# Seven block products for layer 0's values, their sums on GpSimd, and a later load of x

## The chip, the cores and the metric

The kernel runs on one core of a Trainium2 chip. A core has a matrix engine (TensorE, PE in the profile; PEld are its weight loads), a vector engine (VectorE, DVE), an engine for pointwise functions (ScalarE, ACT), a general one (GpSimd, POOL) and one that here only issues transfers (SyncE, SP). Each works through its own instructions in order and waits on semaphores for the others. Matrix products land in PSUM, everything else lies in SBUF. The metric is the device time of one execution in microseconds, as the median over several runs.

## What is computed

Two attention blocks on x of shape (8, 512, 32, 32): eight elements, 512 channels, 1024 tokens. Everything is fp32. Cut to what matters:

```python
# layer 0, heads of 64 channels
hn = group_norm(x, gn1_scale, gn1_bias)
qkv = einsum('bchw,oc->bohw', hn, w_qkv) + b_qkv      # q, k, v
wgt = softmax(einsum('bct,bcs->bts', q * scale, k * scale))
a = einsum('bts,bcs->bct', wgt, v)
x = x + group_norm(einsum('bchw,oc->bohw', a, w_proj) + b_proj, gn2_scale, gn2_bias)
# layer 1, one head of 512 channels
qkv = einsum('oc,bcn->bon', w_qkv1, x);  qkv = qkv / rms(qkv)
h = softmax(q^T k / sqrt(512)) applied to v
x = (x + einsum('oc,bcn->bon', w_out, h)) / sqrt(2)
```

The change concerns v of layer 0, the product of the normalized input hn (512 channels by 1024 tokens) with 512 x 512 weights.

## The kernel before

The elements go one after the other, and of two neighbours the stages overlap. For one element b there are these stages.

**Steps.** A loop of 32 steps (lines 1151 to 1215; STEPS = 32, NB = 8 steps for each of four pairs of heads). A step takes 128 tokens of one pair of heads. Heads.step (line 595) writes out the order: the softmax of step i (a maximum on VectorE, the exponential on ScalarE), every second step values() (TensorE: probabilities times v for an earlier group of two steps), the fills (mostly a projection for the next pair of heads), the scores of step i + 1 on TensorE, turn() (VectorE transposes the probabilities of step i − 1 in blocks of 32, SP sends them on in four transfers into the buffer pT), scale() (GpSimd multiplies the probabilities of step i by their reciprocal sums), and last the list `later`. The probabilities' transposed tiles pb have two buffers, so a transposition waits until the transfers of two steps before have landed.

**Drain.** Lines 1217 to 1241 and finish_layer0 (line 781): the last two values(), the last turn(), then the output projection with its group norm and the residual. Into it the values of the next element are laid as fills for TensorE: project_v0 (line 505) yields eight pieces, each the four 128x512 matmuls of 128 tokens against the weights near["v"], with one copy by ScalarE for two pieces. One piece stands ahead of values(14), three ahead of values(15), the other four in finish_layer0 around the norm's small matmuls. The output projection's weights proj7 are fetched behind the last turn(); x's four loads are issued in steps 28 and 30 and two ahead of values(15).

**Layer 1.** Layer1.project (line 840) starts with the products py of x and the matrix gram, goes on with the score units, the value units and the weight units; then come the products with e and the output.

Several matrix products are made from seven block products instead of eight (class Seven, line 697; in the manner of Strassen and Winograd): an operand is cut into 2 x 2 blocks; the left sums S1 to S4 of the weights are prepared once in the prologue (operands, line 1043), the right sums T1 to T4 of the data are made by RightSide.sums (line 674), eight VectorE subtractions of 128x512. A unit is seven products of two matmuls each. Two products share one PSUM tile of two banks, and when both are issued, their drains follow: for the first product a copy by ScalarE, for the others adds on VectorE, two for the fifth. In the order of the products the fourth is A22 times T4. Before, layer 0's output projection, layer 1's scores, values and weights are made so; layer 0's values are not. Layer 0's projections for queries and keys have a form of their own (Sums and project_seven).

**What sets the order.** InOrder (line 26) pins every instruction in program order on its engine, and so SP's transfers too: what is written later waits behind what is written earlier. Big SBUF tiles come from seven slots (Slots, line 37): a slot given back goes to the end of the list, and the next taker waits for its last reader. Weights live in four named places of one buffer each (places, line 213): "qk", "v", "p" and parts of them; a fetch into a place waits for the last reader of what stood there. The PSUM pool ps_s has three tiles of two banks, tag "sc", which the scores, the seven-product pairs and py share in turn. In the place "v", 3,584 columns wide, near["v_"] is the part that holds v's weights and, at another time, sums of hn (t3); near["v#"] is the rest and serves as scratch space for project_rows and project_seven.

Of the kernel before, what the change touches and what calls it, by code (L numbers as in the profile page):

```python
# [13 lines left out]
P = 128  # L14
# [38 lines left out]
def attention_blocks_kernel(  # L53
# [153 lines left out]
    def rsqrt(r, v, n, name):  # L207
# [4 lines left out]
    CH = C // 2  # L212
    places = {
        "qk": ("qk", [P, 2, CI, C]), "score": ("qk", [P, 7, 2, CH]), "qk7": ("qk", [P, 2, 14, P]),
        "v": ("v", [P, 7, 2, CH]), "value": ("v", [P, 7, 2, CH]),
        "proj": ("p", [P, CI, C]), "gram": ("p", [P, CI, C]), "t24": ("p", [P, CI, HN]), "proj7": ("qk", [P, 7, 2, CH]),
    }
    far = {
        name: dram.tile([P, CI, C] if name == "v" else shape, F32, tag=f"far_{name}", name=f"far_{name}")
        for name, (_, shape) in places.items()  # L220
        if name not in ("qk", "t24", "qk7")
    }

    far["qk0"] = dram.tile([P, 2, CI, P], F32, tag="far_qk0", name="far_qk0")
# [4 lines left out]
    def place(name, b):  # L229
        tag, shape = places[name]  # L230
        near[name] = weights.tile(shape, F32, tag=f"w_{tag}", name=f"{name}_{b}")
        if name == "v":

            flat = near[name].rearrange("p k h c -> p (k h c)")
            near["v#"], near["v_"] = flat[:, CI * C :], flat[:, : CI * C]
            near[name] = flat[:, : CI * C].rearrange("p (ci c) -> p ci c", ci=CI)
        return near[name]
# [139 lines left out]

        return qk, pieces()

    def project_rows(b, j, hn):  # L380

        qk = pair.tile([P, 2, N], F32, tag="qk", name=f"qk_{b}_{j}")
        kp = qk[:, 1, :].rearrange("p (be m) -> p be m", be=4)
        spare = near["v#"]

        def pieces():
            for t in (1, 0):

                w = near["qk"][:, t, :, j * P : (j + 1) * P] if b < 2 else near["qk0"][:, t]
                bias = col(BK, j) if t else bqs[:, j : j + 1]
                for th in range(2):
                    hs = slice(th * HN, (th + 1) * HN)
                    pms = [bank(f"pqk_{b}_{j}_{t}_{th}_{r}") for r in range(2)]
                    for ci in range(CI):
                        for r in range(2):
                            PE.matmul(
                                pms[r],
                                w[halves[r], ci, :],  # L400
                                hn[halves[r], ci, hs],
                                start=(ci == 0),
                                stop=(ci == CI - 1),
                            )
                    to, rest = qk[:, 0, hs], spare[:, hs]
                    if t:

                        to = kp[:, :, th * P : (th + 1) * P]
                        rest = rest.rearrange("p (be m) -> p be m", be=4)
                        pms = [pm.rearrange("p (m be) -> p be m", be=4) for pm in pms]  # L410
                    AC.activation(to, pms[0], AF.Identity, bias=bias)
                    AC.copy(rest, pms[1])
                    yield [lambda to=to, rest=rest: PO.tensor_add(to, to, rest)], []

        return qk, pieces()
# [89 lines left out]
    def project_v0(b, hn, v):  # L505

        for t2 in range(NT // 2):
            pm = wide(f"pv0_{b}_{t2}")
            for k in range(2):
                t = 2 * t2 + k  # L510
                run(matmuls(pm[:, k, :], [(hn[:, ci, t * P : (t + 1) * P], near["v"][:, ci, :]) for ci in range(CI)]))
                if k:
                    AC.copy(v[:, 2 * t2 : 2 * t2 + 2, :], pm)
                yield

    class Heads:
        def __init__(self, b, hn, v, qk):
# [149 lines left out]
    class RightSide:  # L667
# [3 lines left out]
        def __init__(self, xt, t12, t34):  # L671
            self.xt, self.t12, self.t34 = xt, t12, t34

        def sums(self, j):

            xt, t12, t34 = self.xt, self.t12, self.t34
            m, (t1, t2) = j % 2, (slice(0, HN), slice(HN, N))
            if j < 2:
                VE.tensor_sub(t12[:, 0, m], xt[:, m, t2], xt[:, m, t1])
            else:  # L680
                VE.tensor_sub(t12[:, 1, m], xt[:, j, t2], t12[:, 0, m])
                VE.tensor_sub(t34[:, 0, m], xt[:, j, t2], xt[:, m, t2])
                VE.tensor_sub(t34[:, 1, m], xt[:, j, t1], t12[:, 1, m])

        def columns(self, cols):

# [94 lines left out]
    def finish_layer0(b, h, rhs, xt, v0):  # L781

        o, w = big(f"o_{b}"), near["proj7"]
        st = small.tile([P, CI, 2, 6], F32, tag="gn_st2", name=f"st2_{b}")
        mv = small.tile([P, CI, 2], F32, tag="gn_mv2", name=f"mv2_{b}")
        norm = GroupNorm(mv, CI, G2S, G2B, f"2_{b}")

        def unit(m):
            c = {
                f"{i + 1}{th + 1}": o[:, m + 2 * i, th * HN : (th + 1) * HN] for i in range(2) for th in range(2)  # L790
            }
            return Seven(
                f"o_{b}_{m}", HN,
                lambda k, hh: w[:, k, hh, m * P : (m + 1) * P], rhs.columns(slice(0, HN)), c, lambda which: None,
                bias=(col(BP, m), bpd[:, m : m + 1]),
            ).steps()

        def stats(j):
            for k in range(2):
                gn_stats(st[:, j], o[:, j, :], k)  # L800

        units = [unit(m) for m in range(2)]
        for u in units:
            next(u)

        for j in range(CI // 2 + 1, CI):
            rhs.sums(j)
        for m, u in enumerate(units):
            for k in range(6):
                next(u)  # L810
                if k == 3:
                    stats(m + 2)
            stats(m)
        slots.give(f"a_{b}")
        slots.give(f"ta_{b}")
        fetch("score", b)
        next(v0)
        for j in range(CI):
            VE.bn_aggr(mv[:, j, :], st[:, j])
        norm.means()  # L820
        next(v0)
        a, c = norm.coeffs()
        for j in range(CI):
            AC.activation(o[:, j, :], o[:, j, :], AF.Identity, bias=c[:, j : j + 1], scale=a[:, j : j + 1])
            VE.tensor_add(xt[:, j, :], xt[:, j, :], o[:, j, :])
        run(v0)
        slots.give(f"o_{b}")

    class Layer1:
# [188 lines left out]

    def turn_w0(t, name):
        turn(w0rows[t], near["v"] if t == 2 else near["qk"][:, t], name, QSCALE0 if t == 0 else 1.0)  # L1020
        if t == 2:
            SY.dma_start(out=far["v"], in_=near["v"])

    def operands_qk():

# [90 lines left out]
    turn_w0(2, "v")  # L1116
    for ci in range(CI):
        norm1.apply(ci, PO if ci % 2 else VE)
    operands("score", score, [block.tile([P, 4, 2, CH], F32, tag="pb", name=f"score7_{i}") for i in range(2)])
    for ci in range(CI):  # L1120
        AC.copy(value[:, ci, :], product(wv, [woT[:, o, :] for o in range(CI)], ci, "pB"))
# [26 lines left out]
    for b in range(B):  # L1148
        hn, more = heads.hn, b + 1 < B
        todo, due, rest = iter(()), [], []  # L1150
        for i in range(STEPS):
# [13 lines left out]
                fill, later = fills[i] + fill, laters[i]  # L1165
            if r == 0:
                if j + 1 < CI:
                    heads.qk[j + 1], todo = project_seven(b, j + 1, one.next.right) if b else project_rows(b, j + 1, hn)
                elif more:
                    qk_next, todo = project_rows(b + 1, 0, hn_next)  # L1170
                if j + 1 == CI:
                    slots.give(f"hn_{b}")
                    if not more:
                        o_last = big(f"o_{b}")
                        todo = project_out_half(b, heads, o_last)
# [28 lines left out]
            if b and i == STEPS - NB - 3 and not more:  # L1204
                fetch("proj", b)
            m, odd = divmod(i - STEPS + NB, 2)
            if b and more and m in (0, 1) and not odd:
                near["v"] = near["v_"].rearrange("p (ci c) -> p ci c", ci=CI)
                SY.dma_start(out=near["v"][:, 2 * m : 2 * m + 2], in_=far["v"][:, 2 * m : 2 * m + 2])

            if i == STEPS - 4:
                xt = big(f"x_{b}")
            if m in (2, 3) and not odd:
                load_x(b, xt, m - 2)
            heads.step(i, fill, early, later)

        if more:
            v0_next = big(f"v0_{b + 1}", NT)
            v0 = project_v0(b + 1, hn_next, v0_next)
            next(v0)  # L1220
        heads.values(STEPS // RG - 2)
        heads.turn()
        if more:
            fetch("proj7", b)
            if b:
                fetch("gram", b)
            ta = big(f"ta_{b}").rearrange("p (k i) (h n) -> p k i h n", k=2, h=2)
            rhs = RightSide(heads.a, ta[:, 0], ta[:, 1])
            for j in range(CI // 2 + 1):
                rhs.sums(j)  # L1230
            for _ in range(3):
                next(v0)
        else:
            fetch("score", b)
            begun = OutBegun(b, heads)
        for ci in (2, 3):
            load_x(b, xt, ci)
        heads.values(STEPS // RG - 1)
        slots.give(f"v0_{b}")
        if more:  # L1240
            finish_layer0(b, heads, rhs, xt, v0)
        else:
            finish_last(b, heads, xt, o_last, begun)
# [81 lines left out]
```

## Time and profile before

| | us |
|---|---|
| median of 3 runs | 3268.25 |
| lowest, highest | 3268.03, 3272.53 |
| profiled execution | 3268.6 |
| its span, first to last instruction | 3266.5 |
| mean granted TensorE clock | 0.998 |

The page gives for every engine the time in which it had work, then groups of like instructions: source line (all go through one helper, so all have line 34), engine, operation, output <- inputs, partitions x elements, count; behind the first bar the busy time in us and the mean length in ns; behind the second the idle time before them and what ended it. Tile names are short: pv is the PSUM tile of layer 0's values (and of the norm's second small matmul), po that of values(), p_o, p_u, p_v and p_e are the seven-product pairs of the output projection, the scores, the values and the weights, with _B for a product with a plain block and _T for one with a sum. A timeline line has the start in us, the length, the engine, the operation and the count of merged instructions. A line of a windows table has a stretch, its length, the busy time (and count) of PE, PEld, DVE, ACT and POOL, the granted clock, the busy share of the DMA engines and GB/s. The prologue ends at about 102 us; an element takes about 395 us.

Waits in total that touch the drain, from the table of waits: TensorE on pT's transfers 4.9 us in 5 places, VectorE's transposition on pT's transfers 24.6 us in 17.

### The profile page before, as it was taken

What the parts mean: (1) busy time and instruction counts of PE and PEld (TensorE: products, weight loads), DVE (VectorE), ACT (ScalarE), POOL (GpSimd) and SP (SyncE); (2) the same over time, 40 slices, a digit from 0 to 9 for tenths busy, and PEclk for the clock granted to TensorE, in tenths of its full rate; (3) what the DMA queues carried; (4) which work ended last, traced back from release to release, by engine and by line L of the source; (5) the groups of instructions that cost most, each with busy time, mean ns of one, the idle gap of its engine ahead of it and who ended that gap; (6) DMA issues with size and microseconds to landing.
All of it is one profiled execution on the core that took longest, in us unless ns stands there. A gap on an engine that the chain in (4) does not pass through costs nothing.

```text
span 3266.5 us, 35730 instructions
## 1 busy us (share of the span) xinstructions
PE 3235.1 (99%) x13010; PEld 1597.2 (49%) x13010; DVE 2229.7 (68%) x2982; ACT 1064.6 (33%) x1813; POOL 1127.6 (35%) x945
## 2 busy tenths in 40 slices
PE   8999999999999999999999999999999999999899
PEld 5444544445444454544544445444454545444354
DVE  5696667855678556885668756686667866568643
ACT  2453114521145211551215412254123531145210
POOL 0552124611256112660227503264123721246121
PEclk9999999999999999999999999999999999999999
DMA  6776215852168511783228822388214862157500
GB/s 190 212 202 171 74 48 155 220 179 58 49 181 224 164 42 55 205 230 121 52 77 213 228 84 58 98 217 235 73 50 113 216 201 74 23 155 211 180 7 26
DMA packets 228981, 438.88 MB, mean 134 GB/s; under 512 B 28708, under 2 KB 69192, under 8 KB 223048
## 3 DMA queue, kind: packets, MB, share of 16 engines
q1 hardware_dynamic: 228688, 436.58, 47.9%
q8 instruction: 104, 1.70, 0.2%
q14 instruction: 69, 0.57, 0.0%
q10 hardware_dynamic: 120, 0.02, 0.0%
HBM read 125.46 MB, written 28.74 MB: 47 GB/s over the span
## 4 chain that ended last, share of the span: by engine, by line
PE 90%; DMA 4%; DVE 3%; SPq 2%; issue 1%; POOL 0%; DVEq 0%; ACT 0%; ACTq 0%; POOLq 0%
PE po L34 25%; PE s L34 12%; PE pv L34 7%; PE p_e_T L34 7%; PE pq L34 6%; PE p_e_B L34 5%; PE py L34 4%; PE pqk L34 4%; DMA pT<-pb 4%; PE p_u_T L34 3%; PE p_v_T L34 3%; PE p_o_T L34 3%; PE p_v_B L34 3%; PE p_u_B L34 3%; PE p_o_B L34 2%; DVE pb L34 2%
## 5 line engine op out<-in xcount | busy, mean ns | idle before, releaser
L34 ACT ACTIVATE p<-s,nm 128x1024 f32<-128x1024 f32 x512 | 565.5, 1109 | 886.3 <-DVE nm L34 803.2
L34 POOL TENSOR_SCALAR p<-p,tt 128x1024 f32<-128x1024 f32 x512 | 565.9, 1118 | 812.7 <-DVE tt L34 798.4
L34 DVE TENSOR_REDUCE nm<-s 128x1 f32<-128x1024 f32 x512 | 602.3, 1218 | 160.2 <-PE s L34 160.0
L34 DVE STREAM_TRANSPOSE pb<-p 128x2048 f32<-128x2048 f32 x256 | 589.8, 2304 | 42.6 <-DMA pT<-pb 24.6
L34 PE MATMUL s<-qk 64*128 64x512 f32 x2048 | 523.6, 604 | 0.8 <-ACT p L34 0.2
L34 PE MATMUL po<-pT,v 128*64 128x256 f32 x4096 | 470.3, 382 | 4.9 <-DMA pT<-pb 4.9
L34 PE MATMUL po<-e,v 128*128 128x512 f32 x1024 | 451.7, 595 | 0.0
L34 PEld LDWEIGHTS po<-pT,v 128*64 128x64 f32 x4096 | 285.4, 137 | 227.2 <-ACT v L34 53.8
L34 POOL TENSOR_TENSOR u<-u,xy 128x512 f32<-128x512 f32 x64 | 78.9, 1269 | 764.5 <-DVE u L34 470.9
L34 PEld LDWEIGHTS s<-qk 64*128 64x128 f32 x2048 | 198.8, 186 | 252.0 <-issue 229.4
L34 PEld LDWEIGHTS po<-e,v 128*128 128x128 f32 x1024 | 191.9, 190 | 245.0 <-issue 236.4
L34 PE MATMUL pv<-v,hn 128*128 128x512 f32 x512 | 229.0, 598 | 0.0
L34 PE MATMUL pq<-hn,qk 64*128 64x512 f32 x504 | 197.1, 592 | 0.0
L34 ACT ACTIVATE e<-e,shift,rinv 128x512 f32<-128x512 f32 x128 | 100.9, 812 | 257.0 <-DVE e L34 257.0
L34 POOL TENSOR_TENSOR esum<-esum,e 128x512 f32<-128x512 f32 x96 | 130.4, 1360 | 154.2 <-ACT e L34 151.7
L34 DVE TENSOR_TENSOR e<-e,p_e_T 128x512 f32<-128x512 f32 x160 | 107.0, 685 | 86.9 <-PE p_e_T L34 84.7
L34 POOL TENSOR_TENSOR qk<-qk,v 128x512 f32<-128x512 f32 x124 | 162.8, 1320 | 3.2 <-ACT v L34 1.6
L34 PE MATMUL pqk<-hn,qk 64*128 64x512 f32 (+1 forms) x672 | 158.2, 590 | 0.0
L34 PEld LDWEIGHTS pv<-v,hn 128*128 128x128 f32 x512 | 94.6, 190 | 115.1 <-issue 114.3
L34 PE MATMUL pq<-t,qk 64*128 64x512 f32 x336 | 150.9, 589 | 0.0
L34 PE MATMUL pq<-v,qk 64*128 64x512 f32 x336 | 150.9, 589 | 0.0
L34 PE MATMUL p_e_T<-s,t 128*128 128x512 f32 x320 | 147.8, 592 | 0.0
(206 smaller groups left out, 3748.4 us busy)
## 6 DMA issues: line engine op xcount, KB each, us to landing
pT<-pb SPq DMA_DIRECT2D x1024, 256.0 KB, 4.6
qk<-far_qk SPq DMA_DIRECT2D x21, 896.0 KB, 8.2
hn<-in_x_dram SPq DMA_DIRECT2D x32, 512.0 KB, 6.1
x<-in_x_dram SPq DMA_DIRECT2D x32, 512.0 KB
out_dram<-x SPq DMA_DIRECT2D x32, 512.0 KB, 4.8
score<-far_score SPq DMA_DIRECT2D x8, 1792.0 KB
value<-far_value SPq DMA_DIRECT2D x8, 1792.0 KB, 7.5
proj<-far_proj SPq DMA_DIRECT2D x7, 1792.0 KB
```

The source lines that it names most:

```text
L34: return lambda *args, **kw: self._pin(call(*args, **kw))
```

## The change

Layer 0's values of the next element (elements 1 to 7) come from four units of seven products (project_v7), each product two matmuls of 128x256. v's weights are no longer stored as they are; operands() makes the seven left blocks "v7" in the prologue and stores them, and they are fetched whole, in four parts, in steps 24 to 27, also in element 0. The right sums of hn (tv, a slot taken at step 24) are made by GpSimd, one a step in the last eight steps, at the end of `later`. Of the 28 products, four stand ahead of values(14), ten ahead of values(15), four and two around the norm's means and two ahead of each of the four residual adds. Since v7 fills near["v#"] too, the scratch space of project_rows for the next element moves to a tile "spare" in place "p", and gram is fetched anew in element 0 as well. x's slot is taken, and its four loads issued, behind values(15); in the last element x stays as it was.

```diff
+        "spare": ("p", [P, N]),
...
+    def project_v7(b, right, v):
+
+        w = near["v7"]
+        for m in range(CI):
+            c = {f"{i + 1}{th + 1}": v[:, m + 4 * th, i * CH : (i + 1) * CH] for i in range(2) for th in range(2)}
+            yield from Seven(
+                f"v0_{b}_{m}", CH,
+                lambda k, h: w[:, k, h, :], right(slice(m * P, (m + 1) * P)), c, lambda which: None, swap=True,
+            ).steps()
...
-        def sums(self, j):
+        def sum_steps(self, j, engine=VE):
...
-                VE.tensor_sub(t12[:, 1, m], xt[:, j, t2], t12[:, 0, m])
-                VE.tensor_sub(t34[:, 0, m], xt[:, j, t2], xt[:, m, t2])
-                VE.tensor_sub(t34[:, 1, m], xt[:, j, t1], t12[:, 1, m])
+                engine.tensor_sub(t12[:, 1, m], xt[:, j, t2], t12[:, 0, m])
+                yield
+                engine.tensor_sub(t34[:, 0, m], xt[:, j, t2], xt[:, m, t2])
+                yield
+                engine.tensor_sub(t34[:, 1, m], xt[:, j, t1], t12[:, 1, m])
+                yield
...
         for j in range(CI):
             VE.bn_aggr(mv[:, j, :], st[:, j])
+        products(4)
         norm.means()
-        next(v0)
+        products(2)
         a, c = norm.coeffs()
         for j in range(CI):
+            products(2)
             AC.activation(o[:, j, :], o[:, j, :], AF.Identity, bias=c[:, j : j + 1], scale=a[:, j : j + 1])
             VE.tensor_add(xt[:, j, :], xt[:, j, :], o[:, j, :])
...
-            SY.dma_start(out=far["v"], in_=near["v"])
+    operands("v7", near["v"], [prob.tile([P, 4, 2, CH], F32, tag="p", name=f"v7_{i}") for i in range(2)])
...
-                    qk_next, todo = project_rows(b + 1, 0, hn_next)
+                    qk_next, todo = project_rows(b + 1, 0, hn_next, place("spare", b))
...
-            if b and more and m in (0, 1) and not odd:
-                near["v"] = near["v_"].rearrange("p (ci c) -> p ci c", ci=CI)
-                SY.dma_start(out=near["v"][:, 2 * m : 2 * m + 2], in_=far["v"][:, 2 * m : 2 * m + 2])
-
-            if i == STEPS - 4:
+            if more and m >= 0:
+                if m < 2:
+                    k = slice(2 * (i - STEPS + NB), min(2 * (i - STEPS + NB) + 2, 7))
+                    SY.dma_start(out=near["v7"][:, k], in_=far["v7"][:, k])
+                if i == STEPS - NB:
+                    tv = big(f"tv_{b + 1}").rearrange("p (k i) (h n) -> p k i h n", k=2, h=2)
+                    right_v = RightSide(hn_next, tv[:, 0], tv[:, 1])
+                    sums_v = (None for ci in range(CI) for _ in right_v.sum_steps(ci, PO))
+                later.append(lambda: next(sums_v, None))
...
+            v0 = project_v7(b + 1, right_v.columns, v0_next)
+            for _ in range(4):
+                next(v0)
         heads.values(STEPS // RG - 2)
         heads.turn()
         if more:
             fetch("proj7", b)
-            if b:
-                fetch("gram", b)
+            fetch("gram", b)
...
-            for _ in range(3):
+            for _ in range(10):
                 next(v0)
...
         heads.values(STEPS // RG - 1)
         slots.give(f"v0_{b}")
         if more:
+            xt = big(f"x_{b}")
+            for ci in range(CI):
+                load_x(b, xt, ci)
             finish_layer0(b, heads, rhs, xt, v0)
```

More of the change, by code (lines that the diff above doesn't have):

```diff
@@ L214, in attention_blocks_kernel @@
         "qk": ("qk", [P, 2, CI, C]), "score": ("qk", [P, 7, 2, CH]), "qk7": ("qk", [P, 2, 14, P]),
-        "v": ("v", [P, 7, 2, CH]), "value": ("v", [P, 7, 2, CH]),
+        "v": ("v", [P, 7, 2, CH]), "v7": ("v", [P, 7, 2, CH]), "value": ("v", [P, 7, 2, CH]),
         "proj": ("p", [P, CI, C]), "gram": ("p", [P, CI, C]), "t24": ("p", [P, CI, HN]), "proj7": ("qk", [P, 7, 2, CH]),
+        "spare": ("p", [P, N]),
     }
     far = {
-        name: dram.tile([P, CI, C] if name == "v" else shape, F32, tag=f"far_{name}", name=f"far_{name}")
+        name: dram.tile(shape, F32, tag=f"far_{name}", name=f"far_{name}")
         for name, (_, shape) in places.items()
-        if name not in ("qk", "t24", "qk7")
+        if name not in ("qk", "t24", "qk7", "v", "spare")
     }
@@ L232, in place @@
         if name == "v":
+            near["v7"] = near[name]
             flat = near[name].rearrange("p k h c -> p (k h c)")
@@ L378, in project_qk, with project_rows @@
         return qk, pieces()
-    def project_rows(b, j, hn):
+    def project_rows(b, j, hn, spare):
         qk = pair.tile([P, 2, N], F32, tag="qk", name=f"qk_{b}_{j}")
         kp = qk[:, 1, :].rearrange("p (be m) -> p be m", be=4)
-        spare = near["v#"]
         def pieces():
@@ L678, in sums @@
             if j < 2:
-                VE.tensor_sub(t12[:, 0, m], xt[:, m, t2], xt[:, m, t1])
-            else:
-                VE.tensor_sub(t12[:, 1, m], xt[:, j, t2], t12[:, 0, m])
-                VE.tensor_sub(t34[:, 0, m], xt[:, j, t2], xt[:, m, t2])
-                VE.tensor_sub(t34[:, 1, m], xt[:, j, t1], t12[:, 1, m])
+                engine.tensor_sub(t12[:, 0, m], xt[:, m, t2], xt[:, m, t1])
+                yield
+            else:
+                engine.tensor_sub(t12[:, 1, m], xt[:, j, t2], t12[:, 0, m])
[3 more added lines that the diff above has]
+                engine.tensor_sub(t34[:, 1, m], xt[:, j, t1], t12[:, 1, m])
+                yield
+        def sums(self, j):
+            run(self.sum_steps(j))
         def columns(self, cols):
@@ L816, in finish_layer0, with products @@
         fetch("score", b)
-        next(v0)
+        def products(n):
+            for _ in range(n):
+                next(v0)
         for j in range(CI):
             VE.bn_aggr(mv[:, j, :], st[:, j])
+        products(4)
         norm.means()
-        next(v0)
+        products(2)
         a, c = norm.coeffs()
         for j in range(CI):
+            products(2)
             AC.activation(o[:, j, :], o[:, j, :], AF.Identity, bias=c[:, j : j + 1], scale=a[:, j : j + 1])
@@ L826, in finish_layer0 @@
         run(v0)
+        slots.give(f"tv_{b + 1}")
         slots.give(f"o_{b}")
@@ L1020, in turn_w0 @@
         turn(w0rows[t], near["v"] if t == 2 else near["qk"][:, t], name, QSCALE0 if t == 0 else 1.0)
-        if t == 2:
-            SY.dma_start(out=far["v"], in_=near["v"])
     def operands_qk():
@@ L1167, in attention_blocks_kernel @@
                 if j + 1 < CI:
-                    heads.qk[j + 1], todo = project_seven(b, j + 1, one.next.right) if b else project_rows(b, j + 1, hn)
+                    heads.qk[j + 1], todo = project_seven(b, j + 1, one.next.right) if b else project_rows(
+                        b, j + 1, hn, near["v#"]
+                    )
                 elif more:
-                    qk_next, todo = project_rows(b + 1, 0, hn_next)
+                    qk_next, todo = project_rows(b + 1, 0, hn_next, place("spare", b))
                 if j + 1 == CI:
@@ L1206, in attention_blocks_kernel @@
             m, odd = divmod(i - STEPS + NB, 2)
-            if b and more and m in (0, 1) and not odd:
-                near["v"] = near["v_"].rearrange("p (ci c) -> p ci c", ci=CI)
-                SY.dma_start(out=near["v"][:, 2 * m : 2 * m + 2], in_=far["v"][:, 2 * m : 2 * m + 2])
-            if i == STEPS - 4:
+            if more and m >= 0:
[7 more added lines that the diff above has]
+                later.append(lambda: next(sums_v, None))
+            if not more and i == STEPS - 4:
                 xt = big(f"x_{b}")
-            if m in (2, 3) and not odd:
+            if not more and m in (2, 3) and not odd:
                 load_x(b, xt, m - 2)
@@ L1218, in attention_blocks_kernel @@
             v0_next = big(f"v0_{b + 1}", NT)
-            v0 = project_v0(b + 1, hn_next, v0_next)
-            next(v0)
+            v0 = project_v7(b + 1, right_v.columns, v0_next)
+            for _ in range(4):
+                next(v0)
         heads.values(STEPS // RG - 2)
@@ L1235, in attention_blocks_kernel @@
             begun = OutBegun(b, heads)
-        for ci in (2, 3):
-            load_x(b, xt, ci)
+            for ci in (2, 3):
+                load_x(b, xt, ci)
         heads.values(STEPS // RG - 1)
@@ L1240, in attention_blocks_kernel @@
         if more:
+            xt = big(f"x_{b}")
+            for ci in range(CI):
+                load_x(b, xt, ci)
             finish_layer0(b, heads, rhs, xt, v0)
```

## The prediction

> **What bounds the kernel now.** I read the busy shares first, then the groups with shapes kept apart, then the timelines of the stage that the change touches (the drain behind the 32 steps of an element), engine by engine, and last the waits.
>
> ```profile
> PE 3235.1 (99%) x13010; PEld 1597.2 (49%) x13010; DVE 2229.7 (68%) x2982; ACT 1064.6 (33%) x1813; POOL 1127.6 (35%) x945
> ...
> L34 PE MATMUL pv<-v,hn 128*128 128x512 f32 x512 | 229.0, 598 | 0.0
> L34 PE MATMUL p_v_T<-value,t 128*128 128x256 f32 x448 | 101.9, 379 | 0.0
> L34 DVE TENSOR_TENSOR v<-v,p_v_T 128x256 f32<-128x256 f32 x160 | 64.4, 419 | 48.9 <-PE p_v_T L34 46.7
> L34 POOL TENSOR_TENSOR v<-v 128x512 f32<-128x512 f32 x21 | 26.8, 1274 | 30.6 <-ACT v L34 30.6
> ...
> 1966.10 1.03 PE L34 MATMUL p_v_B<-value,x 128*128 128x256 f32 x4
> 1990.28 1.88 PE L34 MATMUL p_e_B<-u,x 128*128 128x512 f32 x4
> ```
>
> TensorE has work in 99% of the span: a microsecond of it is a microsecond of the kernel, as long as nothing makes it wait. The records of one matmul overlap, so the mean of 598 ns is no price; the distance between starts is. An fp32 matmul leaves two records (256 matmuls of layer 0's values, 512 records). The last two lines are the first and the next work of layer 1's value units: 28 products of two 128x256 matmuls each, the same shape as what the change puts into layer 0. They fill 1966.10 to 1990.28, 24.18 us, 0.864 us a product.
>
> The drain of element 3 (PE, then POOL, DVE and SP in the same stretch):
>
> ```profile
> 1468.24 3.70 PE L34 MATMUL pv<-v,hn 128*128 128x512 f32 x8
> 1471.87 3.67 PE L34 MATMUL po<-pT,v 128*64 128x256 f32 x32
> 1485.97 3.67 PE L34 MATMUL po<-pT,v 128*64 128x256 f32 x32
> 1489.58 3.70 PE L34 MATMUL p_o_B<-a,proj 128*128 128x512 f32 x8
> 1513.71 3.60 PE L34 MATMUL pv<-v,hn 128*128 128x512 f32 x8
> 1520.81 0.28 PE L34 MATMUL pv<-d,gavg 128*128 128x4 f32 x2
> 1527.89 17.33 PE L34 MATMUL py<-x,gram 128*128 128x512 f32 x40
> 1545.06 1.88 PE L34 MATMUL p_u_B<-x,score 128*128 128x512 f32 x4
> ...
> 1469.46 2.21 POOL L34 TENSOR_SCALAR p<-p,tt 128x1024 f32<-128x1024 f32 x2 [1.71 <-DVE tt L34]
> ...
> 1471.70 2.31 DVE L34 STREAM_TRANSPOSE pb<-p 128x2048 f32<-128x2048 f32 x1 [2.34 <-POOL p L34]
> 1521.12 0.16 DVE L34 TENSOR_SCALAR ve<-pv 128x4 f32<-128x4 f32 x1 [2.90 <-PE pv L34]
> 1524.30 0.16 DVE L34 TENSOR_TENSOR c<-cols,c 128x4 f32<-128x4 f32 x1
> 1525.77 4.63 DVE L34 TENSOR_TENSOR x<-x,o 128x1024 f32<-128x1024 f32 x4 [1.31 <-ACT o L34]
> ...
> 1477.10 1.33 SPq L34 DMA_DIRECT2D proj<-far_proj  x1
> ```
>
> TensorE runs here without a gap: each start follows the work before it. But three chains end close behind it: the last probabilities' scaling (1471.67) and transposition just before values(14) and (15); proj7, whose last packet lands at 1486.5 in the DMA records for a use at 1489.58; and the second norm's chain on VectorE (1521.12 to x's first add at 1525.77), which is done 0.9 us before py starts.
>
> **What the Trainium skill says.** PSUM — Partial Sum Buffer, section The four PSUM rules: GpSimd can't reach PSUM. So the new products' drains stay with VectorE and ScalarE, and only the SBUF sums go to GpSimd; in the trace too no POOL row has a PSUM operand. SBUF — State Buffer, Who interferes with whom: a VectorE instruction with at most one SBUF input and outside its two-port modes doesn't contend with GpSimd. VectorE's work in the steps is of that kind, and the trace agrees: STREAM_TRANSPOSE lasts 2.30 us also in the window from 1813 to 1824, where POOL is busy for 10.0 of 11 us. Perfetto Trace Analysis, Optimization Strategy: a gap that repeats at the same place can mean that PSUM has run out for the next tile; before, none repeats at py; below I expect one.
>
> **The change, part by part.**
>
> *TensorE's work.* 32 matmuls of 512 columns become 56 of 256. Before, 8 records take 3.43 us (1513.71 to the next group), so 8 pieces take 27.45 us. After, by the twin: 24.18 us. Gain 3.27 us for each of seven elements (0 keeps the old form in the prologue), 22.9 us in all.
>
> *GpSimd's last sum against the fourth product.* The eight sums go one to a step behind scale(). Steps 24 to 30 hide them: POOL has 5.7 of 10.7 us busy there, and a sum of about 1.3 us (rows 1.27 to 1.36) fits before the next scale. The last one, T4's second half, is queued behind scale(31), which ends at 1471.67, so it ends at 1472.95. The fourth product (A22 with T4) needs it as weights in its second matmul. TensorE would be there at 1468.24 + 2.59 + 0.43 = 1471.26; it waits 1.7 us and ends at 1473.4. With the 0.2 us that values() showed before its start, values(14) starts at 1473.65 instead of 1471.87. Behind it all of TensorE waits. Then 3.61 us of values, ten products of 0.864 and 0.2, and 3.61 us of values: p_o_B at 1489.7 against 1489.58. The fourteen products done by then should have gained 1.64 us; the wait has eaten it: +0.1 us. Where a wait for pT stood at this place before (0.31 us in element 1, 0.74 in element 4) it is swallowed: 1.05 us back once.
>
> *What waits behind the drains on VectorE.* The drains of products three and four (two adds of 0.42 us) stand ahead of the transposition of step 31, and can't start before 1473.6. It moves from 1471.70 to 1474.5. values(15) needs its transfers only at 1486. But SP issues proj7 behind those four transfers: 1479.9 in place of 1477.10. From issue to the last byte proj7 took 8.9 to 10.5 us in the seven elements: 1488.8 to 1490.4, needed at 1489.7. Cost 0 to 0.7 us an element; x's two loads that lay ahead of it are gone, so I take 0.1.
>
> *The norm chain and PSUM behind the o units.* Let E be their end (1513.71). Fourteen products remain: 12.1 us, plus the two small norm matmuls, so py could start at E + 12.4 (before: 14.2). VectorE: statistics and aggregates to E + 3.2, three drains to 4.5, means to 5.25 (pv<-d at 5.3, hidden), then three drains (6.7) stand ahead of ve; its chain takes 3.34 (1521.12 to 1524.46): c at 10.1. A drain and o's ACT 1.31: x's adds of 1.14 follow at 11.4, 13.3, 15.7 and 17.7, each behind the two or three drains of a pair (0.4 each). All three PSUM tiles of the pool are in turn held by these pairs: py(0) takes the tile of pair two, free at 13.4, and py(1) that of pair three, free at 15.75. So py(0) starts 1.0 us late, py(1) another 0.6. From there TensorE is in front with 3.43, 5.15 and 6.87 us: the u units start at E + 31.2, before E + 31.35. Of 1.7 us gained, 0.15 is left.
>
> *DMA.* v7's four loads come one in each of steps 24 to 27 (0.5 MB, the last 0.25), in place of v's in 24 and 26 and x's in 28 and 30; element 0 gets v7 and a gram load anew. The same pattern stands in the trace: hn's four loads in steps 4 to 7 of element 0:
>
> ```profile
> 146.00:151.00 5.00, 5.00 (x32) 2.23 (x30) 4.92 (x6) 3.35 (x6) 1.39 (x3) 1.00 0.96 292
> 162.00:167.00 5.00, 5.00 (x36) 2.62 (x34) 4.79 (x5) 2.71 (x5) 3.16 (x4) 1.00 0.96 297
> ```
>
> The DMA engines are at 0.96, TensorE is busy for all of both windows: cost 0, up to 0.5 us an element if SP's issues fall behind. x's four loads start when values(15) has freed a buffer (about 1489) and have until E + 11.4: hidden. gram is due at E + 13: hidden. If that cover went, py would wait for them.
>
> *Prologue.* Four DVE adds of 0.69 us and three POOL copies, where DVE is idle from 61 to 70.7; far_v's store is larger by 0.8 MB. TensorE has no gap there: 0. The move of spare from near["v#"] to a tile of its own adds no instruction.
>
> *Sum.* Per element +0.1 +0.1 −0.15, say 0; two more waits an element, each with a restart of about 0.1 us (an estimate from the 0.03 to 0.2 us between releaser and start in these rows): +1.4 us in seven; −1.05 once. The profiled execution took 3268.6 (span 3266.5 and 2.1 around it), so 3269.0; it lies 0.35 above the median of 3268.25, which leaves 3269 as the forecast.
>
> **The rivals.**
> A, the gain is given back as above: 3269, own range 3263 to 3274.
> B, faster: one of the two waits isn't there, because a PSUM tile is handed on by halves, or GpSimd's last sum is ready sooner. For it: the DVE times are sums of small terms. Against: one tile has one release, and scale(31) has a time in the trace. Either wait is worth 1.6 to 1.8 us an element: 3269 − 7 × 1.7 = 3257; without both 3246.
> C, slower: proj7 decides. Its margin is nil by my sum; if it takes its longest (10.5 us) each time and the transposition comes 0.5 us later than I have it, TensorE waits 1.2 us an element before p_o_B: 3269 + 8.5 = 3278. At its longest it decides once it is issued less than 10.5 us ahead of its use, in element 3 after 1479.2 (my sum: 1479.9). For it: the row in SP's queue, behind the transfers of step 31. Against: less traffic ahead of it.
> D, the products are bound by weight loads (190 ns a load against 216 ns a record) and gain less than the twin: in the twin there is no gap. Slower too, 3275; 3 in 100.
>
> **How the numbers follow.** No change can be told from one within 0.2%, 6.5 us. A 0.43, B 0.27, C with D 0.30. Range 3257 to 3279: A with the nearer part of B and of C.
>
> **What would show it.** Right: pv's fourth product waits for GpSimd in every drain, 1.5 to 2 us; the transposition of step 31 starts about 6 us behind the first product; py waits for VectorE's drains twice, together 1.3 to 2 us; py starts about 13.4 us behind the o units; v0's products are 0.864 us apart. Wrong: no wait at py, or one for proj7 over 0.5 us, or PE gaps in steps 24 to 27.

## The result and the profile after

| | before | after |
|---|---|---|
| median of 8 runs, us | 3268.14 | 3278.28 |
| lowest, highest | 3265.82, 3272.53 | 3271.48, 3282.40 |
| profiled execution (its span) | 3268.6 (3266.5) | 3280.76 (3278.6) |

The ratio is 1.003, with an interval from 1.0019 to 1.0041: 10 us slower. TensorE's work has become less, and the kernel is longer all the same. The page of the kernel after has, where before's had 3235.1 us of TensorE:

```profile
PE 3223.2 (98%) x13346; PEld 1661.9 (51%) x13346; DVE 2304.4 (70%) x3182; ACT 1046.7 (32%) x1813; POOL 1200.7 (37%) x1004
```

TensorE is busy for 11.9 us less in a span 12.1 us longer: 24 us more in which it has nothing to do. Who made it wait stands in the table of waits (engine, tile, what was waited for; total in us, times, longest). None of these rows is in the table of before:

```profile
PE py L34 <- DVE v L34: 10.2, 14, 1.2
PE p_v_T L34 <- POOL tv L34: 8.5, 6, 1.4
PE p_o_B L34 <- DMA proj<-far_proj: 5.3, 7, 1.4
```

So there are three places, each in all seven elements that take the new form (the table puts the seventh wait for tv down to pT, 1.4 us; py waits twice in each element). The next fence has them in TensorE's timeline of element 3, whose drain starts at 1473.66 and whose o units end at 1519.73:

```profile
1473.66 1.13 PE L34 MATMUL p_v_B<-v,hn 128*128 128x256 f32 x4
...
1475.49 1.46 PE L34 MATMUL p_v_T<-v,tv 128*128 128x256 f32 x6
1478.37 0.70 PE L34 MATMUL p_v_T<-v,tv 128*128 128x256 f32 x2 [1.42 <-POOL tv L34]
1479.00 3.67 PE L34 MATMUL po<-pT,v 128*64 128x256 f32 x32
...
1491.43 3.67 PE L34 MATMUL po<-pT,v 128*64 128x256 f32 x32
1495.62 3.67 PE L34 MATMUL p_o_B<-a,proj 128*128 128x512 f32 x8 [0.52 <-DMA proj<-far_proj]
...
1519.73 1.03 PE L34 MATMUL p_v_B<-v,hn 128*128 128x256 f32 x4
1520.60 1.03 PE L34 MATMUL p_v_B<-v,tv 128*128 128x256 f32 x4
1521.46 1.89 PE L34 MATMUL p_v_T<-v,tv 128*128 128x256 f32 x8
...
1533.77 1.98 PE L34 MATMUL py<-x,gram 128*128 128x512 f32 x4 [1.19 <-DVE v L34]
1536.02 15.72 PE L34 MATMUL py<-x,gram 128*128 128x512 f32 x36 [0.27 <-DVE v L34]
1551.57 1.88 PE L34 MATMUL p_u_B<-x,score 128*128 128x512 f32 x4
```

To be seen: the fourth product's second matmul waits 1.42 us for GpSimd's sum, p_o_B 0.52 us for its weights, and py twice for VectorE, 1.19 and 0.27 us. The products themselves cost what the twin promised: 1519.73, 1520.60, 1521.46 are 0.865 us apart. The other engines in that stretch (GpSimd, VectorE, ScalarE, and SP's issues):

```profile
1474.88 2.21 POOL L34 TENSOR_SCALAR p<-p,tt 128x1024 f32<-128x1024 f32 x2 [0.46 <-DVE tt L34]
1477.05 1.26 POOL L34 TENSOR_TENSOR tv<-hn,tv 128x512 f32<-128x512 f32 x1
...
1479.10 0.87 DVE L34 TENSOR_TENSOR v<-v,p_v_T 128x256 f32<-128x256 f32 x2 [2.59 <-PE p_v_T L34]
1479.90 2.30 DVE L34 STREAM_TRANSPOSE pb<-p 128x2048 f32<-128x2048 f32 x1
1529.63 0.16 DVE L34 TENSOR_TENSOR c<-cols,c 128x4 f32<-128x4 f32 x1
1529.71 0.41 DVE L34 TENSOR_TENSOR v<-v,p_v_B 128x256 f32<-128x256 f32 x1
1531.70 1.22 DVE L34 TENSOR_TENSOR x<-x,o 128x1024 f32<-128x1024 f32 x1 [1.58 <-ACT o L34]
...
1530.16 0.37 ACT L34 COPY v<-p_v_B 128x256 f32<-128x256 f32 x1 [8.12 <-DVE v L34]
1530.42 4.64 ACT L34 ACTIVATE o<-o,c,a 128x1024 f32<-128x1024 f32 x4
...
1485.64 1.40 SPq L34 DMA_DIRECT2D proj<-far_proj  x1
```

The last sum is queued behind scale(31) and starts as that ends (1477.05). The transposition of step 31 starts behind two drains, at 1479.90 (6.24 us behind the drain's first product, where it was 3.46), and proj7 goes out behind its transfers, at 1485.64.

Measured from the drain's first product (S) and from the end of the o units (E), before, forecast and after in element 3:

| | before | forecast | after |
|---|---|---|---|
| values(14) starts, S + | 3.63 | 5.41 | 5.34 |
| transposition of step 31, S + | 3.46 | 6.26 | 6.24 |
| proj7 is issued, S + | 8.86 | 11.66 | 11.98 |
| p_o_B could start (values(15) done), S + | 21.34 | 21.46 | 21.38 |
| p_o_B starts, S + | 21.34 | 21.56 | 21.96 |
| x's first add, E + | 12.06 | 11.4 | 11.97 |
| py starts, E + | 14.18 | 13.4 | 14.03 |
| score units start, E + | 31.35 | 31.2 | 31.84 |

From S to the score units the seven elements take 538.9 us before and 547.0 after: +8.05. The other 4.1 us of the 12.1 between the two spans lie ahead of the first drain (282.25 to 283.61), in the steps between (1908.1 to 1910.5 for six) and behind the last (537.2 to 537.5). I take most of these 4.1 for scatter: a second kernel with the old form of v (the run with x's loads moved, below) has 283.3, 1907.9 and 537.2, and the nine other kernels with the new form lie between 282.5 and 283.3, 1906.8 and 1910.3, 535.7 and 540.3. On average those nine take 0.9 us more in these three stretches than the two with the old form. What scatters was not traced.

### The profile page after: what moved, and what is told of

Its sections match the earlier page's. It is cut to its first block, busy times and chain, and to the rows that moved or that the text cites. A ratio compares the mean times of both kernels' runs of the same rounds, so it can differ in the third digit from the quotient of the medians.

```text
span 3278.6 us, 36790 instructions
## 1 busy us (share of the span) xinstructions
PE 3223.2 (98%) x13346; PEld 1661.9 (51%) x13346; DVE 2304.4 (70%) x3182; ACT 1046.7 (32%) x1813; POOL 1200.7 (37%) x1004
## 5 line engine op out<-in xcount | busy, mean ns | idle before, releaser
L34 DVE TENSOR_TENSOR v<-v,p_v_T 128x256 f32<-128x256 f32 x300 | 120.5, 418 | 84.4 <-PE p_v_T L34 80.3
L34 PE MATMUL py<-x,gram 128*128 128x512 f32 x320 | 144.2, 607 | 16.2 <-DVE v L34 10.2
L34 POOL TENSOR_TENSOR qk<-qk,v 128x512 f32<-128x512 f32 x96 | 127.0, 1332 | 3.2 <-ACT v L34 1.6
```

Of the source, the lines that this page charges most:

```text
L34: return lambda *args, **kw: self._pin(call(*args, **kw))
```

## The experiments

My theory: three waits, each with its own cause, took the gain back and more; each can be taken away alone. The rivals: that they are one chain, so that removing one only moves the wait; that GpSimd is too slow for the sums, so that they belong elsewhere; and that x's later loads, not the products, cost the time. Edits are against the kernel after, and "before" in each ratio is the kernel before on the same chip (medians 3268.95, 3268.42 and 3269.59 in the three groups of runs). The kernel after itself ran where before took 3268.14, so a difference between medians of two groups is uncertain by up to 1.5 us from the groups alone; where that matters, the distance of each kernel from its own group's kernel before is given too (the kernel after: 10.1 us above).

**GpSimd's last sum.** In two of the steps (25 and 27) two of the eight sums are issued in place of one, so that the last is done in step 29:

```diff
-                later.append(lambda: next(sums_v, None))
+                for _ in range(2 if i in (STEPS - NB + 1, STEPS - NB + 3) else 1):
+                    later.append(lambda: next(sums_v, None))
```

> GpSimd's last sum of hn is done in step 29 in place of 31 (two sums in steps 25 and 27). Theory 1, the wait for the sum is a price of its own: values(14) starts 3.65 us behind v0's first product in place of 5.34, the transposition of step 31 at about 4.5 us in place of 6.24; proj7 is issued as much earlier as it is needed earlier, so its wait stays; 1.7 us in each of seven elements, 3278 becomes 3266. Theory 2, proj7's landing or the DMA traffic sets the end of the drain: the wait for proj7 grows by what the wait for the sum loses, and the time stays within 3 us of the changed kernel's.

3266.93 us, ratio 0.9992 (0.9986 to 0.9999): 11.4 us below the kernel after. In TensorE's timeline of element 3:

```profile
1467.84 1.13 PE L34 MATMUL p_v_B<-v,hn 128*128 128x256 f32 x4
...
1469.67 1.89 PE L34 MATMUL p_v_T<-v,tv 128*128 128x256 f32 x8
1471.49 3.67 PE L34 MATMUL po<-pT,v 128*64 128x256 f32 x32
...
1488.72 3.67 PE L34 MATMUL p_o_B<-a,proj 128*128 128x512 f32 x8 [1.12 <-DMA proj<-far_proj]
```

The wait for tv is gone (values(14) at S + 3.65 in six elements, 3.80 in the seventh), and the drain up to values(15) has moved up by 1.69 us. The wait ahead of p_o_B stays; it comes to 7.6 us in seven elements, where it was 5.3. So the two are in the main not one chain: with the sums earlier the transposition and proj7's issue come earlier too, and proj7's margin hardly changes (9.45 us in place of 9.40). Of the 11.8 us that the first wait gives back in the trace (seven times 1.69), some 2.4 go to the second; whether by the change or by the scatter of proj7's loads isn't shown.

The same sums on VectorE, `right_v.sum_steps(ci, VE)`, in their old steps:

> The changed kernel with hn's eight sums by VectorE instead of GpSimd at the same places, one a step. If GpSimd's queue (scale of step 31 ahead of the last sum) makes the wait of 1.7 us: the wait goes, values(14) at 3.65 us, as with the earlier sums: 3267. Rival: VectorE, idle for only 0.5 to 0.9 us a step, is pushed past TensorE by a sum of 0.6 to 0.7 us: gaps on TensorE in steps 24 to 31, 3272 to 3278.

3267.05 us, ratio 0.9996 (0.9988 to 1.0004), values(14) at S + 3.65 in six elements again. VectorE has no scale(31) ahead of the last sum. What decides is thus the place of the last sum in a queue: on GpSimd, where a sum takes as long as before, two steps earlier does as well.

**ScalarE ahead of x's first add.** In the tail of finish_layer0 two products stand ahead of each activation that an add of x waits for; in the first of these pairs the second product is drained by a ScalarE copy, so the copy stands ahead of the first activation. The order is turned:

```diff
         for j in range(CI):
-            products(2)
             AC.activation(o[:, j, :], ..., bias=c[:, j : j + 1], scale=a[:, j : j + 1])
+            products(2)
             VE.tensor_add(xt[:, j, :], xt[:, j, :], o[:, j, :])
```

> In the norm's tail o's ScalarE activation is issued ahead of the pair of products, so ahead of the pair's ScalarE copy. Theory 1: x's first add starts 11.4 us behind the o units in place of 12.0, py 13.45 in place of 14.03, the u units 31.25 in place of 31.84: 0.6 us in each of seven elements, 3278 becomes 3274. Rival, PSUM tiles are freed by other terms than this copy: py starts within 0.2 us of 14.03, no change.

3273.79 us, ratio 1.0012 (1.0005 to 1.0018): 4.5 us below the kernel after. py starts at E + 13.47 and the score units at E + 31.23, where the forecast had 13.4 and 31.2. ScalarE and TensorE in element 3 (E is 1517.85 here):

```profile
1527.94 1.24 ACT L34 ACTIVATE o<-o,c,a 128x1024 f32<-128x1024 f32 x1 [7.80 <-DVE c L34]
1529.09 0.35 ACT L34 COPY v<-p_v_B 128x256 f32<-128x256 f32 x1
...
1529.49 2.00 PE L34 MATMUL p_v_B<-v,hn 128*128 128x256 f32 x8 [0.66 <-ACT v L34]
...
1533.54 15.72 PE L34 MATMUL py<-x,gram 128*128 128x512 f32 x36 [0.27 <-DVE v L34]
```

The activation now waits for c alone. The copy behind it is later for it, and the last pair of products waits 0.66 us for the PSUM tile that this copy frees. The wait at py is 0.27 in place of 1.46 us; of the 1.19 saved, 0.6 stay.

**proj7's place in SP's queue.** fetch("proj7", b) goes ahead of the drain's first products, so that it isn't behind step 31's transfers:

> proj7's load is issued ahead of v0's first products, so ahead of the four transfers of step 31 in SP's queue. Theory 1: TensorE's wait of 0.2 to 1.5 us before p_o_B goes (5.3 us in seven elements by the table of waits), nothing else moves: 3278 becomes 3273; the spread of the runs narrows. Rival: step 31's transfers now land behind proj7 and values(15) waits in its place: same time or up to 5 us slower.

3276.41 us, ratio 1.002 (1.0013 to 1.0027), an interval that overlaps that of the kernel after: a gain of 1.9 us (2.7 against its own group's before) can't be told from none. The wait of p_o_B is gone, and most of the gain with it: the rival of the expectation came true. SP and TensorE in element 3:

```profile
1475.79 1.70 SPq L34 DMA_DIRECT2D proj<-far_proj  x1
1479.98 4.32 SPq L34 DMA_DIRECT2D pT<-pb  x4
...
1489.83 3.67 PE L34 MATMUL po<-pT,v 128*64 128x256 f32 x32 [0.57 <-DMA gram<-far_gram]
1493.43 3.70 PE L34 MATMUL p_o_B<-a,proj 128*128 128x512 f32 x8
```

proj7's 1792 KB now stand ahead of the four transfers of 256 KB that values(15) needs, and values(15) waits in place of p_o_B: it starts up to 1.08 us later than S + 17.77, in six of the seven elements (in one of them, by 0.11 us, because values(14) is late). The row puts the wait down to gram, issued next, but in the DMA records gram's last packet ends at 1492.27, after the start at 1489.83; the last packet of pT ends at 1489.27. It is pT that is waited for.

**All three together**, sums, activation and proj7's early fetch:

> All three edits together. Theory 1, the three prices add up: 12 + 5 + 4 = 21 us less than the changed kernel, 3257, which is 11 us under the kernel before. Theory 2, DMA traffic in steps 24 to 27 sets the time: no more than 5 us less than the changed kernel.

3273.95 us, ratio 1.0015 (1.0008 to 1.0022), 17 us above what I expected. The waits for tv, for proj7 and the longer of the two at py are gone, but values(15) has become the place where time is lost:

```profile
1472.73 1.67 SPq L34 DMA_DIRECT2D proj<-far_proj  x1
1475.20 3.83 SPq L34 DMA_DIRECT2D pT<-pb  x4
...
1482.58 1.89 PE L34 MATMUL p_v_B<-v,hn 128*128 128x256 f32 x8
1486.63 5.36 PE L34 MATMUL po<-pT,v 128*64 128x256 f32 x32 [2.16 <-DMA pT<-pb]
1491.92 3.70 PE L34 MATMUL p_o_B<-a,proj 128*128 128x512 f32 x8
```

The transfers are all issued by 1479.03 and values(15) could start at 1484.40; it starts at 1486.63. In the seven elements it starts at S + 17.7 to 18.5, where it was at 16.09 with the sums alone, and p_o_B at S + 21.3 to 23.6. This is what the expectation had left out: the earlier the drain runs, the less room there is for 1792 KB ahead of those transfers.

A second loss stands in the same fence: values(15) takes 5.29 us here, from 1486.63 to 1491.92, in place of 3.61. From 1487.65 on the granted TensorE clock is 0.50 for 3.41 us. The same is seen in elements 1 and 5 (from 695.76 and 2279.54), 5.0 us in all. In no other trace of this document is the clock lowered between the first drain and the last; and 8 of the 18 executions of this kernel have a mean clock of 0.996, which no execution of another kernel here has. What lowers the clock isn't shown: values(15) waits in the other four elements too, 1.3 to 2.3 us, and runs at full clock there. Without the early fetch, sums and activation alone:

> The two edits that paid alone, GpSimd's sums done by step 29 and o's activation ahead of the pair, without the move of proj7. If the prices add up: 3266.9 less 7 times 0.6, 3263. If it was these two that disturbed each other in the run with all three, and not proj7's load, it stays near 3270 or above.

3262.28 us, ratio 0.9978 (0.997 to 0.9987). So the early fetch costs 11.7 us there (11.1 with each kernel against its own group's before). Between the two traces it is 13.9 us from S to the score units, of which the lowered clock has 5.0.

**proj7 in two transfers.** It stays in its old place, but its first block, the only one that p_o_B's first product reads, is a transfer of its own:

```diff
-            fetch("proj7", b)
+            w7 = place("proj7", b)
+            for k in (slice(0, 1), slice(1, 7)):
+                SY.dma_start(out=w7[:, k], in_=far["proj7"][:, k])
```

Alone, then together with sums and activation:

> The changed kernel with nothing but proj7 in two transfers, A11's block first. If the three prices are independent of each other: the wait before p_o_B (5.3 us in seven elements in the changed kernel's profile) goes, all else stays at 5.34, 6.24 and 31.84 us: 3273. If proj7 lands late only because the wait for the sum holds up the transfers ahead of it: the wait stays in part, 3276.

> As the last, and proj7 fetched in two transfers at its old place in SP's queue: first the block A11 alone (0.25 MB), then the other six. p_o_B's first two products need A11 only, the next block is due 3.4 us later. If TensorE's wait there is for the last byte of one large transfer: the wait of about 0.9 us an element goes, 3257. Rival: the first small transfer lands no earlier because the transfers of step 31 and the queue ahead of it set its time: within 2 us of the last.

Alone 3272.71 us, ratio 1.0009 (1.0001 to 1.0017), 5.6 us below the kernel after; p_o_B starts at S + 21.38 in all seven elements. Together 3255.14 us, ratio 0.996 (0.9948 to 0.9973). The drain of element 3 there:

```profile
1461.20 1.13 PE L34 MATMUL p_v_B<-v,hn 128*128 128x256 f32 x4
...
1477.28 3.67 PE L34 MATMUL po<-pT,v 128*64 128x256 f32 x32
1480.89 3.70 PE L34 MATMUL p_o_B<-a,proj 128*128 128x512 f32 x8
```

p_o_B starts at S + 19.69 and waits for nothing; before it was 21.34. The three prices, 11.4, 4.5 and 5.6, sum to 21.5 us, and 3278.28 − 21.5 = 3256.8: they add up to what was measured together, within 1.7 us. Against each group's own kernel before they are 12.2, 5.3 and 7.0, together 24.5, and 23.4 was measured: within 1.1 us. Each of these three intervals lies below that of the kernel after.

**x's loads.** The kernel before with nothing but x's loads moved behind values(15) (and its slot taken there), the last element apart:

> The kernel before, with only x's four loads moved behind values(15) as in the change. Theory: no one waits for x there, and the two waits for pT in elements 1 and 4 (1.05 us) may go: 3268, within 2 us of before. Rival: x in the drain delays gram or the score weights: py or the score units wait, 3272 or more.

3268.88 us, ratio 1.0002 (0.9993 to 1.001). This part of the change costs nothing and brings nothing that can be told. In its trace the small waits for pT at values(14) in elements 1 and 4 are absent (S + 3.63 in all).

**What is left at the end of the drain.** py still waits 0.27 us behind the pairs' drains and x's adds on VectorE. In the last kernel x's second and fourth add go to GpSimd, which does nothing there:

```diff
-            VE.tensor_add(xt[:, j, :], xt[:, j, :], o[:, j, :])
+            (PO if j % 2 else VE).tensor_add(xt[:, j, :], xt[:, j, :], o[:, j, :])
```

> The version with earlier sums, o's activation first and proj7 in two transfers, and x's second and fourth residual add on GpSimd, which is idle there. If VectorE's row of drains and adds sets py by PSUM tiles that come free late: the third and fourth pair are drained 1.1 us sooner; py(1) starts up to 0.9 us sooner, the u units 0.5 to 0.6: 3255 less 4, 3251. Rival: py's second product waits for GpSimd's slower add (about 2.4 us, estimated from 1.27 us for half the columns): same time or up to 4 us slower.

3253.35 us, ratio 0.9949 (0.9935 to 0.9962), the fastest kernel of all. Its interval overlaps that of the run before it; in the trace the score units start at E + 30.70 in place of 31.25 in every element, 3.8 us in seven. TensorE, GpSimd and VectorE in element 3:

```profile
1517.71 17.39 PE L34 MATMUL py<-x,gram 128*128 128x512 f32 x40
...
1517.05 5.66 POOL L34 TENSOR_TENSOR x<-x,o 128x1024 f32<-128x1024 f32 x2 [53.22 <-ACT o L34]
...
1516.74 2.18 DVE L34 TENSOR_TENSOR v<-v,p_v_T 128x256 f32<-128x256 f32 x5
1518.84 1.66 DVE L34 TENSOR_TENSOR x<-x,o 128x1024 f32<-128x1024 f32 x1
1521.09 2.17 DVE L34 TENSOR_TENSOR t<-x 128x512 f32<-128x512 f32 x1
```

py runs through its 40 records without a gap. GpSimd is slower at an add (2.37 and 3.33 us for the two, against 1.22), and the two engines hold each other up, which the last section comes back to.

## Why the prediction was right, and where it was wrong

The forecast was 3269, the gain given back; it came to 3278.28. That is inside the range (to 3279), but outside A's own range (to 3274), and at the number of rival C, on the slower side that had 0.30. That C's number was met is in part luck: C put 8.5 us on proj7 alone, and by the runs proj7 has 5.6 and the norm's tail, which C doesn't name, 4.5. One of the prediction's own signs of being wrong came too: the wait for proj7 is over 0.5 us in five of the seven elements.

*The gain on TensorE*: right. 0.865 us a product against 0.864 from the twin, so 22.9 us were gained and 33 lost. The runs account for the 33: 11.4 (sums), 5.6 (proj7) and 4.5 (ScalarE) by single edits, 3.8 by the adds on GpSimd, by the trace; and 7.4 are still in the tail of the fastest kernel, where the score units start at E + 30.70, and at 29.65 if all of the forecast's 1.7 us less work had come through; no run takes these away. Together 32.7, as close as can be asked of prices that move by 3 us in sum with the median that they are held against.

*GpSimd's last sum*: right in mechanism and size, 5.34 against 5.41, and worth 11.4 us in all, which is seven times 1.63.

*DMA in the steps, x's and gram's loads*: costed at nothing, and so it is: the table of waits has no row for x, gram or v7. In the window of v7's first loads (busy time and count of PE, PEld, DVE, ACT, POOL, then clock, DMA share and GB/s) the DMA engines reach 0.94, and TensorE has work throughout:

```profile
1441.60:1452.30 10.70, 10.70 (x66) 5.22 (x64) 9.27 (x9) 6.15 (x13) 8.16 (x8) 1.00 0.94 285
```

*proj7*: here a term of the sum was mis-sized. I had 8.9 to 10.5 us for a load against a margin of 9.8, and took 0.1 us an element because x's loads were gone from ahead of it. The margin was 9.40 (issue at S + 11.98, needed at S + 21.38; in element 4 only 8.30, since the issue came at S + 13.08). In the DMA records the load took 9.1 to 10.1 us to its last packet, where it was 8.9 to 10.5 before: the lighter traffic gave nothing back. And p_o_B doesn't start with the last packet but some 0.5 us behind it in every element (1495.10 and 1495.62 in element 3), where my sum had 0.1 for a restart. So p_o_B is 0.23 to 1.47 us late, 0.8 on average, 5.7 in seven in place of 0.7. The split shows it: it takes this wait alone away and gains 5.6. Rival C named this mechanism and its point of decision (issued less than 10.5 us ahead of its use); it priced it at 1.2 us an element.

*The norm's tail*: the second mis-sized term, in "a drain and o's ACT 1.31: x's adds follow at 11.4". I let the activation start as c is there. But on ScalarE the copy of the pair just issued stands ahead of it, and this copy isn't free to run when c is done: in the trace it waits for VectorE's drain of the pair's other product, which stands behind c (1529.71, with the copy at 1530.16 in the fence above). The two products share a PSUM tile and write different columns of v; why the copy has to wait for that drain no run shows. So o starts at 1530.42, 0.6 us late, x's first add is at E + 11.97, and every later step of the tail with it: py 14.03 in place of 13.4, the score units 31.84 in place of 31.2. 0.64 us in seven elements is 4.5 us; the activation ahead of the copy brings 4.5 us. That it is this wait, and not the pace of VectorE's adds, is shown by the turned order; what else was predicted of this tail (py's two waits, in the order of 1.3 to 2 us together) came as said, 1.46.

*The restarts*, 1.4 us: too high for values(14), which shows none beyond its wait, and too low for p_o_B, where the 0.5 us are counted in the wait above.

In sum from S to the score units: forecast +0.7 us (7 x 0.05 + 1.4 − 1.05), measured +8.05. proj7 adds 5.0 to the forecast, the tail 4.5; the restarts' own term takes 1.4 off, and the rest, some 0.1 us an element, lies in values(15) ending at S + 21.38 in place of 21.46.

What stays open: the 4.1 us between the two profiled executions that lie outside the drains are taken for scatter because nine kernels with the same steps show 0.9 on average, but no run isolates them. And it isn't shown why proj7's load takes up to 1 us longer in some elements than in others. gram's load, issued right behind it, moves beside it: in the DMA records 71 to 108 of gram's 128 packets start before proj7's last one has ended. In the run with the order of copy and activation turned there are two elements in which only 47 and 35 do, and there proj7 takes 7.9 us and p_o_B doesn't wait. A load of gram issued later would have tested whether that is the cause; no run has it.

## What to carry to other kernels

When work on the bounding engine is replaced by less work and more helpers, list for each helper what is already in its queue at that place: here a copy, a sum and a load behind older work on ScalarE, GpSimd and SP took back 21.5 us against a gain of 22.9, and each was undone by changing only the order or the cut. A load whose length and margin are equal within the spread cost 0.8 us a time here and not the 0.1 of its better cases; the 0.5 us from its last packet to the product that uses it belong into the sum. And moving the large load to an earlier place charged what it then stood ahead of; cutting off the part that is used first was the cheaper way.

## What was not expected of the hardware

A product that reads one seventh of a loaded tile waits until the whole load has landed: 0.23 to 1.47 us here, and nothing once that seventh (256 KB) was a transfer of its own, though proj7 left SP at the same place in both (S + 11.92 and 11.98 in element 3). This fits what the Trainium skill states (DMA: Bandwidth & Descriptors, section Why a DMA increments its semaphore by 16 and not by 1): only the full count means that all of the data has landed. The second issue cost SP less than a microsecond (2.06 us for both in the split alone, 1.40 for the one after), and nothing waited for it.

VectorE's instructions with two SBUF inputs and GpSimd's adds hold each other up in the last kernel: x's add takes 1.66 us in place of 1.22, and a subtraction of 128x512 2.17 in place of 0.68; it ends 0.55 us behind GpSimd's second add (1523.26 against 1522.71). GpSimd pays too: its second add, with VectorE's beside it, takes 3.33 us, its first 2.37. These lengths look like two engines that take turns. The five drains in the same stretch, which have one input in PSUM, keep their 0.42 us (2.18 for five). This is what the Trainium skill states (SBUF — State Buffer, section Who interferes with whom): a VectorE instruction with two SBUF inputs contends with a GpSimd instruction that reads SBUF, because its second input comes through the read interface that the two share; with at most one SBUF input, and outside the two-port modes, it doesn't.
